# A graph network on one Trainium2 core: order of the first loads, places of side work in the first pairs, and the last pair's scores transposed by TensorE

## The chip, the core and the metric

The kernel runs on one core of a Trainium2 chip. The metric is device time in microseconds, lower is better: the median of three executions. A further execution was taken with the hardware profiler, and everything said about instructions comes from that one.

The engines are called as the profile calls them: PE (matmul; PEld is its weight load), DVE (VectorE), ACT (ScalarE), POOL (GpSimd), SP (SyncE, which here only issues DMAs). PSUM is the memory into which PE writes, SBUF the working memory.

## The reference

Two layers work on x of 64 x 256 x 512 with one 256 x 256 adjacency of zeros and ones. Cut to what is computed:

```
h   = relu(layernorm(x))
q, k, v = h Wq', h Wk', h Wv'
rel = adj' * (q k')                  # 256 x 256 per batch
rel = rel / norm(rel, axis=2)        # by row
x   = x + rel v
h   = relu(layernorm(x))
x   = x + (adj h) weight + bias
```

## The kernel before

**Tiling.** Two batches make a pair: 512 tokens, four chunks of 128 tokens on the partitions. There are 32 pairs, and x of a pair lives in one of five ring buffers of 1 MB. Wq and Wk are folded into one matrix m = Wq' Wk in `before_pairs`, so the scores are (h m) h'. Large products go through `winograd`: seven products of 2 x 2 blocks instead of eight, each of eight PE instructions, gathered in three PSUM banks (bank_a, bank_b, bank_c). After each product `take` moves its bank: the first time of a block as a copy on ACT, later as an add on DVE. The operands of products 3 to 7 are sums of blocks that DVE makes (`left_operands`, `right_operands`; four steps each). With `early=True` the product into bank_b is issued second instead of sixth.

**Stages of a pair.** `ln0` makes statistics (DVE) and relu (ACT). h is transposed: for pair 0 by PE (`transposes_by_matmul`), for later ones by 16 DMAs that place blocks of 32 (`place_blocks`, on SP) and DVE transposes within the blocks (`transpose_blocks`), then four sums. `project_g` is h m, `project_v` is h Wv'. `scores` makes rel; side steps mask it by adj' (DVE), make square sums (ACT), square root (ACT) and reciprocal (DVE), scale it (ACT), place it by 16 DMAs on SP, and turn it on DVE. `attend` multiplies turned rel with v and adds to x on DVE, `ln1` normalises again, `gather` multiplies with adj' and `mix` with the second weight and adds.

In `gather` h is split into an upper and a lower part of a shorter float type (`upper` on ACT, `lower` on DVE), which goes with `adjt_r`, adj' cast to that type. This is the branch for an adj whose values the short type holds exactly, chosen at run time: `look` masks the low bits of adj on DVE, reduces them, and leaves `low_any`, which all engines load before the branch.

**Order.** Everything from `before_pairs` on is issued in the order of the program on PE, DVE and ACT; no scheduler moves it. Each `winograd` takes a dict `side`: the steps in slot n are issued after the take of product n. So the place of a step in these dicts is its place in the queue of its engine. [...]

**Around the change.** SP issues wq in four pieces, then x of pair 0, wv, x of pairs 1 and 2, weight, x of pairs 3 and 4 (L99 to L113); ACT issues wk in four pieces; POOL issues adj first (L97) and the bias last (L114), and makes the identity between. `before_pairs` starts PE on 14 matmuls of zeros (L498), then makes the operands of m in the order of L541. The look and the transposes of adj stand in slot 2, those of Wv in slot 5. `first_pairs` is the hand-made order of pairs 0 to 3 until the steady loop can start: `attend(0)` is followed by `project_g(2)` with pair 1's masks and squares in its slots, the cast to `adjt_r` (L629), `gather(0)` with pair 3's sums, and `mix(0)` with `early=True`. `steady` is the loop over pairs 1 to 28. `last_pairs` does the rest: the last pair's scores are scaled and placed in slots of `mix(a)` (L696), turned in `gather(b)` (L697), and used by `attend(c)` (L699).

Of the kernel before, what the change touches and what calls it, by code (L numbers as in the profile page):

```python
# [9 lines left out]
F32 = mybir.dt.float32  # L10
# [9 lines left out]
def kernel(  # L20
# [36 lines left out]
    nc = tc.nc  # L57
# [27 lines left out]

    def load(i):
        X[i] = ring[i % len(ring)]
        nc.sync.dma_start(out=X[i], in_=xs[i])

# [6 lines left out]
    bias_bc = const.tile([P, D], F32, name="bias_bc")  # L96
    nc.gpsimd.dma_start(out=adj_sb, in_=adj.rearrange("(c p) n -> p c n", p=P))  # L97
    for e in range(DC):
        nc.sync.dma_start(out=wq_sb[:, e], in_=wq[e * P : (e + 1) * P, :])  # L99
        nc.scalar.dma_start(out=wk_sb[:, e], in_=wk[e * P : (e + 1) * P, :])  # L100
    ident = const.tile([P, P], F32, name="ident")
    make_identity(nc, ident)
    ones = const.tile([P, 1], F32, name="ones")
    nc.gpsimd.memset(ones, 1.0)
    warm = const.tile([P, P], F32, name="warm")
    nc.gpsimd.memset(warm, 0.0)
    load(0)
    nc.sync.dma_start(out=wv_sb, in_=wv.rearrange("(c p) d -> p c d", p=P))
    load(1)
    load(2)  # L110
    nc.sync.dma_start(out=w_sb, in_=weight.rearrange("(c p) d -> p c d", p=P))
    load(3)
    load(4)  # L113
    nc.gpsimd.dma_start(  # L114
        out=bias_bc, in_=bass.AP(tensor=bias.tensor, offset=bias.offset, ap=[[0, P], [1, D]])
    )

# [8 lines left out]
    def right_operands(b, t):  # L126

        sub = nc.vector.tensor_sub  # L130
        steps = [
            lambda: sub(t[1], b(1, 1), b(0, 1)),
            lambda: sub(b(0, 1), b(0, 1), b(0, 0)),
            lambda: sub(t[0], b(1, 1), b(0, 1)),
            lambda: sub(t[2], b(1, 0), t[0]),
        ]
        return {1: b(0, 0), 2: b(1, 0), 3: b(1, 1), 4: t[2], 5: b(0, 1), 6: t[0], 7: t[1]}, steps

# [77 lines left out]
    def product_of_tokens(left, right):  # L216

        def product(bank, n, start):
            for b in range(NB):
                for d in range(HC):  # L220
                    nc.tensor.matmul(  # L221
                        bank[:, ts(b, P)], right[n][:, d, ts(b, P)], left[n][:, d, ts(b, P)],
                        start=(start and b == 0 and d == 0), stop=(d == HC - 1),
                        skip_group_check=True,
                    )
        return product
# [111 lines left out]

    def scores(i, side={}):

# [43 lines left out]
        def each(f):  # L384
            return [(lambda b=b, k=k: f(b, k)) for k in range(NC) for b in range(NB)]

        winograd(product_of_tokens(left, right), take, side)
        return (
            [lambda: mask(0), lambda: mask(1)], each(square_sum), root, inverse, each(scale), place,
            each(turn),  # L390
        )

    def attend(i, side={}):
        rel, v, xt = R.pop(i), flat(V.pop(i)), flat(X[i])
        for b in range(NB):
            for n in range(NC):
                c = b * NC + n
                pm = ps_m.tile([P, 512], F32, tag="pm", name="pu")
                for m in range(NC):
                    nc.tensor.matmul(  # L400
                        pm[:, :D], rel[:, b, m, n], v[:, b * NC + m, :],
                        start=(m == 0), stop=(m == NC - 1),
                    )
                nc.vector.tensor_add(xt[:, c, :], pm[:, :D], xt[:, c, :])  # L404
                run(side.get(c, ()))
# [89 lines left out]
    def before_pairs():  # L495

        pz = ps_m.tile([P, 512], F32, tag="pm", name="pz")
        for _ in range(14):  # L498
            nc.tensor.matmul(pz[:, :P], warm, warm, start=True, stop=True)
        m_left, left_steps = left_operands(  # L500
            work, wq_sb.rearrange("p c (h n) -> p c h n", h=NC), "ys", "m"
        )
        wk_t = work.tile([P, 3, HC, HD], F32, tag="gt", name="wk_t")
        m_factors, right_steps = right_operands(right_blocks(wk_sb), [wk_t[:, n] for n in range(3)])
        low = work.tile([P, NC * N], I32, tag="h", name="low")
        stats, root, end, relus = ln0(0)
# [19 lines left out]
        def transpose_wv():  # L526
            for d in range(DC):
                pt = ps_m.tile([P, 512], F32, tag="pm", name="ptw")
                for e in range(DC):
                    nc.tensor.transpose(pt[:, ts(e, P)], wv_sb[:, e, ts(d, P)], ident)  # L530
                nc.scalar.copy(wvt_sb[:, d, :], pt[:, :D])

        def take(t, k, bank, first):
# [6 lines left out]

        run(left_steps[0:2] + right_steps[0:2])  # L541
        winograd(product_weights_moving(m_left, m_factors), take, {
            0: [],
            1: [left_steps[2], right_steps[2]],
            2: [left_steps[3], right_steps[3], look, transpose_adj],
            3: stats[0:2],
            4: stats[2:4] + [root],
            5: [end] + relus + m_steps[0:3] + [transpose_wv],
            6: m_steps[3:4],
# [31 lines left out]
    def first_pairs(exact):  # L581
# [5 lines left out]
        project_g(0, {  # L587
            0: stats[0:1], 1: stats[1:2], 2: stats[2:4] + [root], 3: [end] + relus,
            4: wv_steps[0:2], 5: wv_steps[2:3], 6: wv_steps[3:4],
# [23 lines left out]
        project_v(1, {  # L613
            0: gs[0:2], 1: gs[2:3] + turned2[0:2], 2: gs[3:4] + turned2[2:4], 3: turned2[4:6],
            4: turned2[6:8], 5: turns[0:2] + relus[0:2], 6: turns[2:4] + relus[2:4],
        })
# [4 lines left out]
        stats, *parts = ln1(0, exact)  # L621
        attend(0, {c: [stats[c]] for c in range(TC)})
        turned3, sums3 = transpose_blocks(3)
        project_g(2, by_slot(layer_1(parts), {
            0: masks[0:1], 1: masks[1:2], 2: squares, 3: [norm_root], 4: [inverse] + scales + [place],
            5: turned3[0:2], 6: turned3[2:6],
        }))
        if exact:
            nc.vector.tensor_copy(adjt_r, adjt_sb)  # L629
        y_steps = gather(0, exact, {0: turned3[6:8], 1: sums3[0:2], 2: sums3[2:3], 3: sums3[3:4]})  # L630
        stats, root, end, relus = ln0(4)
        mix(0, {
            0: y_steps[0:2], 1: y_steps[2:4], 2: stats[0:1], 3: stats[1:2], 4: stats[2:3],
            5: stats[3:4] + [root] + turns[0:2], 6: [end] + turns[2:4] + relus,
        }, early=True)
        place_blocks(4)
# [38 lines left out]
    def last_pairs(exact):  # L675
# [14 lines left out]
        }, tag="h")  # L690
        masks, squares, norm_root, inverse, scales, place, turns = scores(c)
        stats, *parts = ln1(b, exact)
        attend(b, by_slot({n: [stats[n]] for n in range(TC)}, {
            1: masks[0:1], 2: masks[1:2] + squares[0:2], 3: squares[2:4],
        }))
        mix(a, by_slot({0: [norm_root, inverse]}, layer_1(parts), {1: scales + [place]}))  # L696
        y_steps = gather(b, exact, {2: turns[0:2], 3: turns[2:4]})  # L697
        stats, *parts = ln1(c, exact)
        attend(c, {n: [stats[n], y_steps[n]] for n in range(TC)})  # L699
        mix(b, layer_1(parts))  # L700
        y_steps = gather(c, exact)
        mix(c, {0: y_steps[0:2], 1: y_steps[2:4]}, early=True)

# [35 lines left out]
```

## Time and profile before

| | us |
|---|---|
| median of three runs | 1773.24 (1772.54 to 1774.07) |
| the profiled execution | 1774.41 |
| its span, first to last instruction | 1772.6 |
| mean granted PE clock | 0.995 |
| PE busy in the span | 1741.8 |
| ACT busy / DVE busy | 645.9 / 1217.1 |

The span is what the profile divides; 1.8 us of the profiled execution lie around it. Busy times of different engines overlap. A busy PE isn't necessarily PE at full pace: where the granted clock falls, the same instruction takes longer. Bytes moved by DMA in the first fortieth of the span run at a mean of 225 GB/s, afterwards at 24 to 84. The chain that ended last is 94% PE.

### The profile page before, as it was taken

The numbers are of one execution on the slowest core, as the hardware profiler recorded it, in microseconds if no ns is written. First come the engines' busy times: TensorE is split into PE (matmuls) and PEld (weight loads), VectorE is DVE, ScalarE is ACT, GpSimd is POOL, SyncE is SP. The second block draws the span as 40 slices with busy tenths as digits, with TensorE's granted clock in tenths as the row PEclk, the third lists the DMA queues.
The fourth block names the chain that finished last, engine by engine and source line by source line (L and its number), as shares of the span: only waits on it lengthen the run. The fifth ranks groups of instructions, "written<-read, shape, count | busy, mean of one in ns | idle before, by whom it ended". The sixth has DMA issues, their size and how long they took to land.

```text
span 1772.6 us, 23888 instructions
## 1 busy us (share of the span) xinstructions
PE 1741.8 (98%) x8826; PEld 1452.6 (82%) x8826; DVE 1217.1 (69%) x2355; ACT 645.9 (36%) x1391; POOL 201.1 (11%) x169
## 2 busy tenths in 40 slices
PE   8989999999999999999999999999999999999988
PEld 6878888888888888888988888888888888888866
DVE  5767676667776667676667776676766676766545
ACT  3334333434333344242344233343333343333431
POOL 0011110111110111110111100111100111101111
PEclk9999999999999999999999999999999999999999
DMA  6423332233332233332333332333322333321111
GB/s 225 60 37 77 79 83 49 48 84 75 81 70 58 52 82 75 82 61 62 57 81 74 84 57 58 65 79 77 83 53 49 79 76 79 81 52 24 36 36 50
DMA packets 430062, 122.79 MB, mean 69 GB/s; under 512 B 402416, under 2 KB 403440, under 8 KB 429936
## 3 DMA queue, kind: packets, MB, share of 16 engines
q1 hardware_dynamic: 420768, 87.10, 25.9%
q0 software_dynamic: 8592, 33.03, 5.3%
q8 instruction: 71, 1.16, 0.3%
q10 hardware_dynamic: 576, 1.05, 0.2%
q14 instruction: 55, 0.45, 0.1%
HBM read 38.27 MB, written 33.55 MB: 41 GB/s over the span
## 4 chain that ended last, share of the span: by engine, by line
PE 94%; DVE 2%; ACT 1%; SPq 1%; DMA 1%; issue 1%; DVEq 0%; ACTq 0%
PE bank_a L209 25%; PE pu L400 12%; PE bank_c L209 12%; PE bank_a L197 12%; PE py L449 7%; PE bank_a L221 6%; PE bank_c L197 6%; PE bank_b L209 6%; PE bank_c L221 3%; PE bank_b L197 3%; PE bank_b L221 2%; SPq L379 1%; DMA wq_sb<-in_L_gnn_Wq_dram 0%; DVE st L240 0%; ACT h2c L252 0%
## 5 line engine op out<-in xcount | busy, mean ns | idle before, releaser
L400 PE MATMUL pu<-v,turned 128*128 128x512 f32 x512 | 229.4, 601 | 8.9 <-DVE turned L382 6.6
L422 POOL TENSOR_TENSOR x_ring<-x_ring,bias_bc 128x512 f32<-128x512 f32 x128 | 175.0, 1386 | 462.1 <-ACT h2c L252 462.1
L400 PEld LDWEIGHTS pu<-v,turned 128*128 128x128 f32 x512 | 95.5, 192 | 128.0 <-issue 108.6
L240 DVE BATCH_NORM_STATS2 st<-x_ring 128x6 f32<-128x512 f32 x256 | 176.1, 688 | 4.3
L333 ACT COPY v<-bank_a 128x512 f32<-128x512 f32 x96 | 56.0, 583 | 307.3 <-PE bank_a L209 301.0
L430 DVE TENSOR_TENSOR h<-h2c,h 128x512 fp32r<-128x512 f32 x128 | 122.5, 974 | 63.8 <-ACT h L426 63.8
L466 DVE TENSOR_TENSOR x_ring<-bank_a,x_ring 128x512 f32<-128x512 f32 x128 | 87.3, 682 | 90.5 <-PE bank_a L209 86.7
L473 POOL DMA_DIRECT2D out_dram<-x_ring x31 | 23.9, 770 | 1087.6 <-issue 834.9
L316 ACT COPY g<-bank_a 128x512 f32<-128x512 f32 x96 | 56.2, 585 | 220.1 <-PE bank_a L197 219.4
L449 PE MATMUL py<-adjt_r,h 128*128 128x256 f32 x1024 | 128.3, 284 | 3.9 <-DVE adjt_r L629 3.9
L449 PEld LDWEIGHTS py<-adjt_r,h 128*128 128x128 f32 x1024 | 122.8, 192 | 4.4 <-issue 4.3
L209 PE MATMUL bank_a<-w_t,ys 128*128 128x256 f32 x512 | 121.3, 380 | 1.1 <-DVE x_ring L466 1.1
L209 PE MATMUL bank_a<-wv_t,hs 128*128 128x256 f32 x512 | 120.9, 379 | 0.0
L197 PE MATMUL bank_a<-hs,m_t 128*128 128x256 f32 x512 | 120.9, 379 | 0.0
L245 ACT ACTIVATE rs<-rs 128x4 f32<-128x4 f32 x64 | 13.2, 206 | 278.5 <-DVE rs L244 278.5
L252 ACT ACTIVATE h<-x_ring,nb,rs 128x512 f32<-128x512 f32 x124 | 91.0, 803 | 51.4 <-DVE nb L249 51.4
L209 PEld LDWEIGHTS bank_a<-w_t,ys 128*128 128x128 f32 x512 | 97.0, 190 | 15.4 <-DVE x_ring L466 2.3
L404 DVE TENSOR_TENSOR x_ring<-pu,x_ring 128x512 f32<-128x512 f32 x128 | 88.4, 690 | 30.8 <-PE pu L400 23.3
L252 ACT ACTIVATE h2c<-x_ring,nb,rs 128x512 f32<-128x512 f32 x128 | 97.4, 806 | 29.6 <-DVE h L430 15.3
L209 PEld LDWEIGHTS bank_a<-wv_t,hs 128*128 128x128 f32 x512 | 97.3, 190 | 13.2
L197 PEld LDWEIGHTS bank_a<-hs,m_t 128*128 128x128 f32 x512 | 97.3, 190 | 13.2
L453 ACT COPY yt<-py 128x512 f32<-128x512 f32 x128 | 73.9, 578 | 40.6 <-PE py L449 40.6
(149 smaller groups left out, 3250.9 us busy)
## 6 DMA issues: line engine op xcount, KB each, us to landing
x_ring<-in_x_dram SPq DMA_DIRECT2D x32, 1024.0 KB, 5.6
blocks<-h SPq DMA_DIRECT2D x496, 64.0 KB, 2.3
out_dram<-x_ring POOLq DMA_DIRECT2D x31, 1024.0 KB, 5.2
placed<-rel SPq DMA_DIRECT2D x512, 32.0 KB, 2.0
wq_sb<-in_L_gnn_Wq_dram SPq DMA_DIRECT2D x4, 256.0 KB, 6.4
wk_sb<-in_L_gnn_Wk_dram ACTq DMA_DIRECT2D x4, 256.0 KB, 5.6
wv_sb<-in_L_gnn_Wv_dram SPq DMA_DIRECT2D x1, 1024.0 KB, 11.3
w_sb<-in_L_gnn_weight_dram SPq DMA_DIRECT2D x1, 1024.0 KB, 14.4
```

The source lines that it names most:

```text
L197: nc.tensor.matmul(bank[:, e * HT_ : (e + 1) * HT_], right[n][:, d, ts(e, P)], left[n][:, d, :], start=(start and e == 0 and d == 0), stop ...
L209: nc.tensor.matmul(bank[:, b * HD : (b + 1) * HD], left[n][:, d, ts(b, P)], right[n][:, d, :], start=(start and b == 0 and d == 0), stop=( ...
L221: nc.tensor.matmul(bank[:, ts(b, P)], right[n][:, d, ts(b, P)], left[n][:, d, ts(b, P)], start=(start and b == 0 and d == 0), stop=(d == H ...
L240: nc.vector.bn_stats(st[:, c, :], src[:, c, :])
L252: nc.scalar.activation(dst, src[:, c, :], AF.Relu, bias=nb[:, c : c + 1], scale=rs[:, c : c + 1])
L400: nc.tensor.matmul(pm[:, :D], rel[:, b, m, n], v[:, b * NC + m, :], start=(m == 0), stop=(m == NC - 1),)
L404: nc.vector.tensor_add(xt[:, c, :], pm[:, :D], xt[:, c, :])
L422: nc.gpsimd.tensor_tensor(xt[:, c, :], xt[:, c, :], bias_bc, ALU.add)
L430: nc.vector.tensor_sub(dst[:, 1, c, :], whole_h[c], dst[:, 0, c, :].bitcast(F32))
L449: nc.tensor.matmul(pm[:, d, :], left[:, b * NC + m, ts(d0 + d, P)], right, start=(n == 0), stop=(n == len(terms) - 1),)
L453: nc.scalar.copy(y[:, d0 : d0 + 2, :, b, :], pm.rearrange("p d (h n) -> p d h n", h=NC))
L466: nc.vector.tensor_add(xt[block], bank.rearrange("p (b e) -> p b e", b=NB), xt[block])
```

## The change

Five things change.

1. Loads. adj is issued by ACT ahead of wk. SP issues only wq and x of pair 0. wv, x of pairs 1 to 4, weight and bias are issued by ACT, from slots of the m product and of `project_g(0)`. POOL issues no load; it makes ones and the zeros for the warm matmuls first and the identity last.
2. The start of `before_pairs`. A square root of one number comes first on ACT. Eight warm matmuls instead of 14. The look and the transposes of adj come ahead of all operand steps. `right_operands` has a fourth buffer here, so its second step no longer overwrites a block of wk. Steps stand in other slots; of the four copies of Wv's transposes two are on ACT and two on DVE, and they stand ahead of the relus.
3. `first_pairs`. Two relus of pair 3 move from slots 5 and 6 to 2 and 3 of `project_v(1)`. Masks, squares and square root of pair 1 move from `project_g(2)` into `attend(0)`. The cast to `adjt_r` moves ahead of `project_g(2)`. Pair 3's DVE transposes start a slot earlier, its sums move from `gather(0)` to the last slot of `mix(0)`. `mix(0)` is no longer early; two of its operand steps come before it.
4. The last pair. `scores(c)` is not scaled, placed and turned; `turn_at_once` transposes it with eight PE transposes after `mix(a)`, and ACT copies the two banks. `attend(c)` multiplies by the reciprocal norm of the row in its add on DVE.
5. The last `mix` is no longer early; two of its operand steps come before it.

```diff
-    def load(i):
+    def load(i, queue=nc.sync):
         X[i] = ring[i % len(ring)]
-        nc.sync.dma_start(out=X[i], in_=xs[i])
+        queue.dma_start(out=X[i], in_=xs[i])
...
-    nc.gpsimd.dma_start(out=adj_sb, in_=adj.rearrange("(c p) n -> p c n", p=P))
+    nc.scalar.dma_start(out=adj_sb, in_=adj.rearrange("(c p) n -> p c n", p=P))
     for e in range(DC):
         nc.sync.dma_start(out=wq_sb[:, e], in_=wq[e * P : (e + 1) * P, :])
         nc.scalar.dma_start(out=wk_sb[:, e], in_=wk[e * P : (e + 1) * P, :])
-    ident = const.tile([P, P], F32, name="ident")
-    make_identity(nc, ident)
+    load(0)
...
-    load(0)
-    nc.sync.dma_start(out=wv_sb, in_=wv.rearrange("(c p) d -> p c d", p=P))
-    load(1)
-    load(2)
-    nc.sync.dma_start(out=w_sb, in_=weight.rearrange("(c p) d -> p c d", p=P))
-    load(3)
-    load(4)
-    nc.gpsimd.dma_start(
-        out=bias_bc, in_=bass.AP(tensor=bias.tensor, offset=bias.offset, ap=[[0, P], [1, D]])
-    )
+    ident = const.tile([P, P], F32, name="ident")
+    make_identity(nc, ident)
+
+    def load_wv():
+        nc.scalar.dma_start(out=wv_sb, in_=wv.rearrange("(c p) d -> p c d", p=P))
+
+    def load_w_and_bias():
+        nc.scalar.dma_start(out=w_sb, in_=weight.rearrange("(c p) d -> p c d", p=P))
+        nc.scalar.dma_start(
+            out=bias_bc, in_=bass.AP(tensor=bias.tensor, offset=bias.offset, ap=[[0, P], [1, D]])
+        )
...
+        diff = t[3] if len(t) > 3 else b(0, 1)
         steps = [
             lambda: sub(t[1], b(1, 1), b(0, 1)),
-            lambda: sub(b(0, 1), b(0, 1), b(0, 0)),
-            lambda: sub(t[0], b(1, 1), b(0, 1)),
+            lambda: sub(diff, b(0, 1), b(0, 0)),
+            lambda: sub(t[0], b(1, 1), diff),
             lambda: sub(t[2], b(1, 0), t[0]),
         ]
...
+        def turn_at_once():
+            for b in range(NB):
+                pt = ps_m.tile([P, T], F32, tag="pm", name="pr")
+                for t in range(NC):
+                    for k in range(NC):
+                        nc.tensor.transpose(
+                            pt[:, ts(t * NC + k, P)], rel[:, b, k, ts(t, P)], ident
+                        )
+                nc.scalar.copy(turned[:, b].rearrange("p t k n -> p (t k n)"), pt)
...
-                nc.vector.tensor_add(xt[:, c, :], pm[:, :D], xt[:, c, :])
+                if scale is None:
+                    nc.vector.tensor_add(xt[:, c, :], pm[:, :D], xt[:, c, :])
+                else:
+                    nc.vector.scalar_tensor_tensor(
+                        xt[:, c, :], pm[:, :D], scale[:, b, n : n + 1], xt[:, c, :],
+                        op0=ALU.mult, op1=ALU.add,
+                    )
...
+        root_table = small.tile([P, 1], F32, tag="rt", name="root_table")
+        nc.scalar.activation(root_table, ones, AF.Sqrt)
         pz = ps_m.tile([P, 512], F32, tag="pm", name="pz")
-        for _ in range(14):
+        for _ in range(8):
...
-        wk_t = work.tile([P, 3, HC, HD], F32, tag="gt", name="wk_t")
-        m_factors, right_steps = right_operands(right_blocks(wk_sb), [wk_t[:, n] for n in range(3)])
-        low = work.tile([P, NC * N], I32, tag="h", name="low")
+        wk_t = work.tile([P, 4, HC, HD], F32, tag="h", name="wk_t")
+        m_factors, right_steps = right_operands(right_blocks(wk_sb), [wk_t[:, n] for n in range(4)])
+        low = work.tile([P, NC * N], I32, tag="rel", name="low")
...
-                nc.scalar.copy(wvt_sb[:, d, :], pt[:, :D])
+                if d < HC:
+                    nc.scalar.copy(wvt_sb[:, d, :], pt[:, :D])
+                else:
+                    nc.vector.tensor_copy(wvt_sb[:, d, :], pt[:, :D])
...
-        run(left_steps[0:2] + right_steps[0:2])
+        look()
+        transpose_adj()
+        run([right_steps[1], left_steps[0], left_steps[1]])
         winograd(product_weights_moving(m_left, m_factors), take, {
-            0: [],
+            0: [load_wv],
             1: [left_steps[2], right_steps[2]],
-            2: [left_steps[3], right_steps[3], look, transpose_adj],
-            3: stats[0:2],
-            4: stats[2:4] + [root],
-            5: [end] + relus + m_steps[0:3] + [transpose_wv],
+            2: stats[0:2] + [lambda: load(1, nc.scalar)],
+            3: [left_steps[3]] + stats[2:4] + [root, right_steps[0], lambda: load(2, nc.scalar)],
+            4: [transpose_wv, end] + relus + [right_steps[3]],
+            5: m_steps[0:3],
             6: m_steps[3:4],
         }, early=True)
...
         project_g(0, {
-            0: stats[0:1], 1: stats[1:2], 2: stats[2:4] + [root], 3: [end] + relus,
+            0: stats[0:1] + [lambda: load(3, nc.scalar)],
+            1: stats[1:2] + [lambda: load(4, nc.scalar)],
+            2: stats[2:4] + [root, load_w_and_bias], 3: [end] + relus,
...
-            0: gs[0:2], 1: gs[2:3] + turned2[0:2], 2: gs[3:4] + turned2[2:4], 3: turned2[4:6],
-            4: turned2[6:8], 5: turns[0:2] + relus[0:2], 6: turns[2:4] + relus[2:4],
+            0: gs[0:2], 1: gs[2:3] + turned2[0:2], 2: gs[3:4] + turned2[2:4] + relus[0:2],
+            3: turned2[4:6] + relus[2:4], 4: turned2[6:8], 5: turns[0:2], 6: turns[2:4],
...
-        attend(0, {c: [stats[c]] for c in range(TC)})
+        attend(0, by_slot({c: [stats[c]] for c in range(TC)}, {
+            0: masks[0:1], 1: masks[1:2] + squares[0:2], 2: squares[2:4] + [norm_root],
+        }))
         turned3, sums3 = transpose_blocks(3)
-        project_g(2, by_slot(layer_1(parts), {
-            0: masks[0:1], 1: masks[1:2], 2: squares, 3: [norm_root], 4: [inverse] + scales + [place],
-            5: turned3[0:2], 6: turned3[2:6],
-        }))
         if exact:
             nc.vector.tensor_copy(adjt_r, adjt_sb)
-        y_steps = gather(0, exact, {0: turned3[6:8], 1: sums3[0:2], 2: sums3[2:3], 3: sums3[3:4]})
+        project_g(2, by_slot(layer_1(parts), {
+            1: [inverse], 3: scales + [place], 4: turned3[0:1], 5: turned3[1:2], 6: turned3[2:4],
+        }))
+        y_steps = gather(0, exact, {0: turned3[4:6], 1: turned3[6:7], 2: turned3[7:8]})
+        run(y_steps[0:2])
         stats, root, end, relus = ln0(4)
         mix(0, {
-            0: y_steps[0:2], 1: y_steps[2:4], 2: stats[0:1], 3: stats[1:2], 4: stats[2:3],
-            5: stats[3:4] + [root] + turns[0:2], 6: [end] + turns[2:4] + relus,
-        }, early=True)
+            0: y_steps[2:3], 1: y_steps[3:4] + stats[0:1], 2: stats[1:2], 3: stats[2:3],
+            4: stats[3:4] + [root], 5: [end] + turns + relus, 6: sums3,
+        })
...
-        masks, squares, norm_root, inverse, scales, place, turns = scores(c)
+        masks, squares, norm_root, inverse, rn, turn_at_once = scores(c, by_matmul=True)
...
-        mix(a, by_slot({0: [norm_root, inverse]}, layer_1(parts), {1: scales + [place]}))
-        y_steps = gather(b, exact, {2: turns[0:2], 3: turns[2:4]})
+        mix(a, by_slot({0: [norm_root, inverse]}, layer_1(parts)))
+        turn_at_once()
+        y_steps = gather(b, exact)
         stats, *parts = ln1(c, exact)
-        attend(c, {n: [stats[n], y_steps[n]] for n in range(TC)})
+        attend(c, {n: [stats[n], y_steps[n]] for n in range(TC)}, rn)
         mix(b, layer_1(parts))
         y_steps = gather(c, exact)
-        mix(c, {0: y_steps[0:2], 1: y_steps[2:4]}, early=True)
+        run(y_steps[0:2])
+        mix(c, {0: y_steps[2:4]})
```

More of the change, by code (lines that the diff above doesn't have):

```diff
@@ L130, in right_operands @@
         sub = nc.vector.tensor_sub
+        diff = t[3] if len(t) > 3 else b(0, 1)
         steps = [
             lambda: sub(t[1], b(1, 1), b(0, 1)),
-            lambda: sub(b(0, 1), b(0, 1), b(0, 0)),
-            lambda: sub(t[0], b(1, 1), b(0, 1)),
+            lambda: sub(diff, b(0, 1), b(0, 0)),
+            lambda: sub(t[0], b(1, 1), diff),
             lambda: sub(t[2], b(1, 0), t[0]),
         ]
-        return {1: b(0, 0), 2: b(1, 0), 3: b(1, 1), 4: t[2], 5: b(0, 1), 6: t[0], 7: t[1]}, steps
+        return {1: b(0, 0), 2: b(1, 0), 3: b(1, 1), 4: t[2], 5: diff, 6: t[0], 7: t[1]}, steps
     def weight_operands(w, name):
@@ L337, in project_v, with scores @@
         winograd(product_weights_moving(HL[i], wv_right), take, side)
-    def scores(i, side={}):
+    def scores(i, side={}, by_matmul=False):
         left, right = HL.pop(i), G.pop(i)
@@ L385, in each @@
             return [(lambda b=b, k=k: f(b, k)) for k in range(NC) for b in range(NB)]
+        def turn_at_once():
[7 more added lines that the diff above has]
+                nc.scalar.copy(turned[:, b].rearrange("p t k n -> p (t k n)"), pt)
         winograd(product_of_tokens(left, right), take, side)
+        if by_matmul:
+            masks = [lambda: mask(0), lambda: mask(1)]
+            return masks, each(square_sum), root, inverse, rn, turn_at_once
         return (
@@ L391, in scores, with attend @@
         )
-    def attend(i, side={}):
+    def attend(i, side={}, scale=None):
         rel, v, xt = R.pop(i), flat(V.pop(i)), flat(X[i])
```

## The prediction, made before the result was known

> **What bounds the kernel now.** I read first the busy shares, then the list of what the matrix engine (PE) waited for, then PE's instructions in order of time at the head, around pair 0's second layer and at the end, and last the chain of waits and the clock table there. The page:
>
> ```profile
> span 1772.6 us, 23888 instructions
> PE 1741.8 (98%) x8826; PEld 1452.6 (82%) x8826; DVE 1217.1 (69%) x2355; ACT 645.9 (36%) x1391; POOL 201.1 (11%) x169
> ```
>
> PE is the bound, so only time in which PE stands still or runs slowly can be won. The waits of PE over the whole run (total, times, longest):
>
> ```profile
> PE pu L400 <- DVE turned L382: 6.6, 2, 6.2
> PE py L449 <- DVE adjt_r L629: 3.9, 1, 3.9
> PE bank_a L209 <- DVE x_ring L466: 2.7, 5, 0.8
> PE pf L514 <- DVE low_max L512: 2.1, 1, 2.1
> PE bank_c L209 <- DVE yt L159: 1.2, 2, 0.6
> ```
>
> Nothing here repeats by pair: the long waits happen once each, outside the steady loop. PE in order of time (start, duration, what; the bracket is the idle time before):
>
> ```profile
> 17.84 3.45 PE L209 MATMUL bank_a<-wk_t,ys_m 128*128 128x256 f32 x8
> 117.76 6.52 PE L449 MATMUL py<-adjt_r,h 128*128 128x256 f32 x32 [3.91 <-DVE adjt_r L629]
> 163.48 3.90 PE L449 MATMUL py<-adjt_r,h 128*128 128x256 f32 x32
> 1726.48 9.39 PE L400 MATMUL pu<-v,turned 128*128 128x512 f32 x16 [6.20 <-DVE turned L382]
> 1764.83 1.99 PE L209 MATMUL bank_a<-w_t,yt 128*128 128x256 f32 x8 [0.78 <-DVE x_ring L466]
> ```
>
> A product of 8 matmuls normally follows the last by 1.73 us; the one at 17.84 took 3.3, pair 0's gather 6.4 against 3.7 for the same 32 matmuls at 163.48, the last attend 9.2 against 6.87. Each follows a pause. The clock column shows why (PE, PEld, DVE, ACT, POOL busy, then granted clock):
>
> ```profile
> 118.00:120.00 2.00, 2.00 (x10) 2.00 (x11) 1.93 (x4) 0.15 (x1) 0.00 (x0) 0.50 0.40 55
> 1728.00:1730.00 2.00, 2.00 (x3) 0.67 (x2) 0.00 (x0) 0.00 (x0) 0.00 (x0) 0.50 0.00 0
> ```
>
> So a pause costs its length and some 1.5 to 2.6 us of half clock after it. The chain of waits at the head (start, us, what):
>
> ```profile
> 2.18 8.66 DMA wq_sb<-in_L_gnn_Wq_dram
> ...
> 26.53 2.22 ACT blocks L252 x3
> ...
> 29.37 1.86 ACT wvt_sb L531 x4
> ...
> 31.74 2.08 ACT ht L281 x4
> ```
>
> After the last piece of wq (10.84) DVE does its subtractions, then the look at adj, and PE stands behind it; at the end ACT is the bound: four relus, four wvt copies, four ht copies in a row.
>
> [...]
>
> **Head.** In PE's order the products of m = wq'wk write bank_a, bank_b, bank_c, then bank_a, bank_c, bank_a, bank_a again; s and t are the sums of wq and wk that DVE makes for them. Arrivals: about 2.5 MB lie ahead of the last weight piece before and after (adj leaves POOL's queue and goes ahead of wk on ACT's; bias goes away), so that piece still lands at about 10.9 and bank_b, which needs it, still ends at 12.5. adj now has the place of wk's first piece (shortest landing 3.8 us): about 4.6. The look (0.42 + 0.69), its small matmul and four transposes (0.83) end by 7, before bank_a's weights (wk's second piece, some 7.7): hidden, with 1.3 us to spare. In the compiled order wk's fourth issue on ACT waits for adj's completion counter; nothing on ACT is due before 6.9. Then, with a DVE pitch of 0.6 to 0.7, 1.65 for two stats and 1.73 for a product, bank_c starts at 12.5 behind bank_b, no longer at 13.04 behind wk's in-place subtraction, and ends at 14.25.
>
> DVE makes the add of bank_b by 13.4, s[1] by 14.0 and t[0] by 14.65, so the second bank_a product runs from 14.75 to 16.5 (before 17.84 to 21.1, behind the look and at half clock). Two stats end at 16.3, s[2] at 16.95; the second bank_c product runs from 17.05 to 18.8, wv's 16 transposes to 20.7, the last two products to 22.4 and 24.3.
>
> DVE goes on with two stats, the root's input and t[1] to 19.4, the add to 20.0, two wvt copies to 21.6, reciprocal and nb to 21.95. ACT has made the other two wvt copies by 20.6; its relus take 22.0 to 24.9, m_sb ends at 25.5, then ht comes. Before, four wvt copies stood between relus and m_sb.
>
> The first ht copy starts at 25.5, not 31.74: 6.2 us. wv is issued on ACT at some 10.5, behind x0: 2.6 us at 400 GB/s and a landing make 15.5; due 18.8. x1 to x4, w and bias are issued in ACT's waits, 0.4 to 0.5 us each as wk's issues. The table load at 21.93 lay in a wait: 0. Six warm matmuls fewer: 0, or one product at half clock (1.5). Bounds 3.7 (that, and the last piece 1 us later) to 7.5 (that piece 1.3 us earlier).
>
> **Pairs 0 to 2.** Moving two relus of pair 3 ahead removes PE's 0.56 us at 90.14. From project_g(2) at 101.58 to attend(1) at 138.10 are 36.5 us; at full pace 12.1 + 3.7 + 12.1 = 27.9. So 8.6 + 0.56 = 9.2 is there. With adjt_r cast before project_g(2), and squares out of ACT's way, the last low part of h2 is done about when gather starts and half a gather before it is needed; gather runs at full clock. The order of mix(0) changes too: bank_b's product goes from second to sixth, which takes away the 0.61 and 0.78 us waits; the second yt step is done 0.8 us after gather, 1.7 allowed. What is late next: (a) two masks (0.58 each) and the cast (0.32) now sit between attend(0)'s adds and ln1(0): the last pair's attend with two masks ended 0.7 us later than one without; with the cast 1.06, less 0.37 that the square root waited anyway, 0.7. ACT's copy of the second bank of project_g(2) stands behind two relus, and PE's fourth product waits for it: 0.6. (b) The four sums of pair 3 (2.75 us) now stand on DVE between the last take of mix(0) and attend(1)'s adds, after four turns (1.4): DVE reaches the first add 2.3 us late, catches up 0.1 per chunk, and project_v(2)'s fourth product waits about 2.0, as its copy before was just in time (150.1 against 150.19). 9.2 - 0.6 - 2.0 = 6.6. Bounds 4.0 (both stalls double) to 9.2. SP's placing of pair 1 may meet the end of w's load: up to 0.4, within these.
>
> **End.** Removed: four scales on ACT (1.7), sixteen placings on SP (12.6, in the chain from 1711.96 to 1726), four turns. Added: eight PE transposes at 0.12 (ptw: 16 in 1.91) = 0.96 before gather(b), two ACT copies of 0.58 beside the gather. attend(c) starts at 1716.29 + 0.96 + 3.73 = 1720.98 (before 1726.48) at full clock. DVE, not PE, is now late: per chunk add, stats, aggregate, one y step = 2.13 us, so the last y step ends at 1731.5, the take of mix(b)'s first bank at 1732.2; PE wanted that bank at 1731.3: 0.9 of stall instead of the 0.26 before. From there mix(b) repeats the trace (9.27 us to gather(c)): gather(c) at 1741.5 (before 1748.85), mix(c) at 1745.3. There the order with bank_b sixth and two y steps before it has no stall: last take 12.35 us after its start, against 14.19. The last take falls from 1766.87 to 1757.7: 9.2. Bounds: 7.2 if the fused add takes 1.2 us (4 x 0.5), 10.9 if mix(b) waits nowhere (0.9, and 0.7 before its fifth product).
>
> **Sum.** 6.2 + 6.6 + 9.2 = 22.0 of the profiled execution's 1774.41 (span 1772.6, 1.8 around it): 1752.4. The runs' median lies 1.2 lower, 1773.24: 1751.2. The steady loop's PE order and side work are unchanged: 0.
>
> **Rivals.** (1) The stalls come back in part, because the moved work lands where slack is nothing: every lower bound at once, 3.7 + 4.0 + 7.2 = 14.9, 1758.3. For: project_v's copies are just in time already. Against: the steady loop lives with that. (2) More than I count: no new stalls, 27.6, about 1746; against it the DVE rows in (b). (3) Slower: ACT, which evicts most PSUM banks, is held at each load it issues until the load before has landed. Two of SP's loads took 4.11 us and two 7.29 to issue. Six 1 MB loads move to ACT, wv in a wait of 4.5 us, so five count; at the 5.6 us that an x load takes to land, 28.0, and 28.0 - 22.0 = 6.0 slower: 1779.2. It decides from 4.4 us a load. Against: [...] and they are spaced 1.7 us or more. That the change does not do what it says: the instruction lists of all engines show the moved steps, so no.
>
> **How the numbers follow.** Forecast 0.60; rival 1 0.27; rival 2 0.07; rival 3 0.04; 0.02 for no change. Bounds give 1745.6 to 1758.3; for what rival 1 leaves beyond them I take 1745.5 to 1760. A measurement here tells 0.2% (3.5 us) from nothing. Faster 0.94, same 0.02, slower 0.04.
>
> **What would show it.** Right: the first ht copy near 25.5; a gather of pair 0 of 3.7 us with no adjt_r wait; a new wait of about 2 us in project_v(2); pr transposes of about 1 us, then attend(c) in 6.9 us. Wrong: load issues on ACT of over 2 us, half clock in the head, or DVE copies that hold the relus past 23.

## The result and the profile after

| | before | after |
|---|---|---|
| median of the runs | 1772.95 us (4 runs, 1772.54 to 1774.07) | 1753.03 us (4 runs, 1751.17 to 1755.15) |
| profiled execution | 1774.41 us, span 1772.6 | 1753.72 us, span 1751.9 |

The ratio is 0.9887, 95% interval 0.9870 to 0.9904: 19.9 us less, where 22.0 were forecast. The page of the kernel after:

```profile
span 1751.9 us, 23847 instructions
PE 1734.2 (99%) x8822; PEld 1447.8 (83%) x8822; DVE 1216.7 (69%) x2353; ACT 644.6 (37%) x1387; POOL 199.4 (11%) x167
```

PE is still the bound. Of the 20.7 us that the span is shorter, only 7.6 are busy time; the rest is idle time. The waits of PE in the kernel after (total, times, longest):

```profile
PE bank_a L210 <- DMA wk_sb<-in_L_gnn_Wk_dram: 1.9, 1, 1.9
PE bank_a L210 <- DVE x_ring L487: 1.8, 3, 0.9
PE bank_c L210 <- ACT v L334: 1.2, 1, 1.2
PE pf L537 <- DVE low_max L535: 1.2, 1, 1.2
PE pu L415 <- DVE turned L384: 0.9, 2, 0.4
```

The 6.2 us for `turned` and the 3.9 for `adjt_r` are gone. What stands first now was not on the list before: wk's second piece, in the head. PE of the kernel after in order of time, with the places shown of before and the new waits:

```profile
8.81 2.90 PE L210 MATMUL bank_a<-wk_sb,wq_sb 128*128 128x256 f32 x6 [1.91 <-DMA wk_sb<-in_L_gnn_Wk_dram]
11.50 3.28 PE L210 MATMUL bank_b<-wk_sb,wq_sb 128*128 128x256 f32 x8
16.93 1.97 PE L210 MATMUL bank_a<-wk_t,ys_m 128*128 128x256 f32 x8 [0.42 <-DVE wk_t L135]
109.32 3.99 PE L470 MATMUL py<-adjt_r,h 128*128 128x256 f32 x32
138.99 1.99 PE L210 MATMUL bank_c<-wvt_sb,hs 128*128 128x256 f32 x8 [1.21 <-ACT v L334]
152.29 3.89 PE L470 MATMUL py<-adjt_r,h 128*128 128x256 f32 x32
1704.73 1.04 PE L394 MATMUL pr<-ident,rel 128*128 128x128 f32 x8
1709.38 7.03 PE L415 MATMUL pu<-v,turned 128*128 128x512 f32 x16
1720.77 1.99 PE L210 MATMUL bank_a<-w_t,ys 128*128 128x256 f32 x8 [0.91 <-DVE x_ring L487]
```

Pair 0's gather takes 3.99 us instead of 6.52, attend(c) 7.03 instead of 9.39; the product at 16.93 has its full pace again. But two products at 8.81 and 11.50 now run at half pace (2.90 us for 6 records, 3.28 for 8; at full pace 8 take 1.89). The clock table of the kernel after says the same (the number behind POOL's is the granted clock):

```profile
9.00:10.00 1.00, 1.00 (x3) 0.82 (x4) 1.00 (x2) 0.00 (x0) 0.00 (x0) 0.50 1.06 410
110.00:112.00 2.00, 2.00 (x20) 2.00 (x19) 2.00 (x7) 1.35 (x3) 0.00 (x0) 1.00 0.38 51
1710.00:1712.00 2.00, 2.00 (x6) 0.80 (x5) 0.70 (x1) 0.16 (x1) 0.00 (x0) 1.00 0.11 43
```

Full clock in the gather and in the last attend; half clock in the head. Its chain of waits, kernel after:

```profile
1.75 6.92 DMA wk_sb<-in_L_gnn_Wk_dram
8.67 0.14 issue
8.81 2.90 PE bank_a L210 x6
11.71 3.09 PE bank_b L210 x8
...
22.43 1.29 DVE wvt_sb L557 x2
...
25.34 1.99 PE bank_a L210 x8
```

The chain now runs over PE and DVE; the relus and wvt copies of ACT that stood in it before are gone from it.

The same milestones in both traces show where the time came from (starts, us):

| milestone | before | after | gained so far |
|---|---|---|---|
| first ht copy | 31.74 | 28.01 | 3.7 |
| gather of pair 1 | 163.48 | 152.29 | 11.2 |
| gather of pair 29 | 1662.71 | 1650.85 | 11.9 |
| gather of the last pair | 1748.85 | 1730.04 | 18.8 |
| last take | 1766.87 | 1746.16 | 20.7 |

With the end of project_g(0) as the border (its last product starts 3.8 us earlier) that is 3.8 for the head, 7.4 for pairs 0 to 2, 0.7 in the loop and 8.9 at the end, against a forecast of 6.2, 6.6, 0 and 9.2. Three questions follow: are the parts independent, why is the head short, and what are the new waits worth?

### The profile page after: what moved, and what is told of

Same layout as the page of the kernel before. It is cut to its first block, busy times and chain, and to the rows that moved or that the text cites. A ratio compares the mean times of both kernels' runs of the same rounds, so it can differ in the third digit from the quotient of the medians.

```text
span 1751.9 us, 23847 instructions
## 1 busy us (share of the span) xinstructions
PE 1734.2 (99%) x8822; PEld 1447.8 (83%) x8822; DVE 1216.7 (69%) x2353; ACT 644.6 (37%) x1387; POOL 199.4 (11%) x167
## 4 chain that ended last, share of the span: by engine, by line
PE 95%; DVE 3%; ACT 0%; DMA 0%; issue 0%; ACTq 0%; DVEq 0%
PE bank_a L210 25%; PE bank_a L198 12%; PE bank_c L210 12%; PE pu L415 12%; PE py L470 7%; PE bank_a L222 7%; PE bank_b L210 6%; PE bank_c L198 6%; PE bank_c L222 3%; PE bank_b L198 3%; PE bank_b L222 2%; DVE st L241 1%; DMA wk_sb<-in_L_gnn_Wk_dram 0%; DVE x_ring L420 0%; DVE x_ring L487 0%
## 5 line engine op out<-in xcount | busy, mean ns | idle before, releaser
L302 DVE STREAM_TRANSPOSE ht<-blocks 128x256 f32<-128x256 f32 x248 | 87.2, 408 | 1.1 <-DMA blocks<-h 1.1
```

The lines of the kernel that those rows point to most:

```text
L302: nc.vector.transpose(ht[:, d, half].rearrange("p (b n) -> p b n", b=NB), by_half[:, :, half, d])
```

## The experiments

All ratios are to runs of the kernel before on the same chip (its medians there: 1774.71, 1774.49 and 1775.40 us).

**The three parts alone.** The kernel before with one part of the diff each.

> Only the head part (loads behind one another on ACT, adj looked at first, fourth buffer for wk's differences, two wvt copies on DVE); side work of pairs 0 to 2 and the last pair as before. Theory (three independent parts, the head's worth read at the first ht copy): 3.8 us below the kernel before, about 1769.1. Rival (the head's gain is taken back later, because the loads of x1 to x4 now come later): less than 2 us. Rival (the forecast's 6.2 is there and what hid it was elsewhere): 6 us.

> Only the other places for side work of pairs 0 to 2, head and last pair as before. Theory: gain 7.4 us (my forecast counted 6.6): gather of pair 0 without the wait for adjt_r and in about 4.0 us, a wait of project_v(2)'s fourth product of about 1.2. Rival (part of the 7.4 belongs to the head, because loads shifted): under 5.

> Only the last pair's part: its scores turned by PE, the fused multiply-add in attend(c), the last mix not in early order. Theory: gain 9.0 us, fused add 0.75, attend(c) 7.0 without a wait, one wait of 0.9 before mix(b)'s third product. Rival (the tail's gain depends on the rest): more than 2 us away from 9.0. The sum of this and the two others is to be the change's whole 19.9 to 20.7 if the parts are independent.

| part alone | median, us | below before | ratio, 95% interval |
|---|---|---|---|
| head | 1770.46 | 4.3 | 0.9977 (0.9969 to 0.9986) |
| pairs 0 to 2 | 1768.47 | 6.2 | 0.9965 (0.9952 to 0.9979) |
| last pair | 1765.74 | 9.0 | 0.9950 (0.9937 to 0.9964) |

They sum to 19.5 us; the whole change gave 19.9, and 21.4 when it was run again. So they are independent within what these runs tell. The end alone also shows the forecast's path step by step: the last gather starts at 1741.45 and the last take at 1757.70, where 1741.5 and 1757.7 were forecast. Head and pairs give 0.3 and 0.9 us less alone than their own traces show at the gather of pair 1 (4.6 and 7.1). One reason can be read, though it was not tried: both keep the last pair's placing by DMA, and attend(c) waits 6.9 and 6.8 us for it there, 6.2 in the one profile of before. Scatter is as large: the runs of the head alone reach from 1768.07 to 1772.81.

**The clock in the head.** The six warm matmuls that the change takes away, put back:

```diff
-        for _ in range(8):
+        for _ in range(14):
```

> The kernel after, with 14 warm matmuls again in place of 8. Theory (the head fell 2.4 us short of my forecast because fewer warm matmuls, then idle time behind 4.5 and 6.9 us, let PE's clock fall to half for bank_a and bank_b): both at full clock, bank_b's product ends near 12.7 instead of 14.8, first ht copy near 26.0 instead of 28.0, 1.7 to 2.1 us below the kernel after (about 1751.2). Rival (the weights' landing is the bound, the clock only fills the wait): bank_b ends at 14 or later, no gain. Rival (more warm matmuls only delay the look at adj behind them): up to 1 us slower.

Measured: 1752.92 us, ratio 0.9879 (0.9863 to 0.9894). PE of this kernel:

```profile
1.04 5.93 PE L522 MATMUL pz<-warm 128*128 128x128 f32 x28 [1.04 <-POOL warm L105]
...
7.51 1.89 PE L210 MATMUL bank_a<-wk_sb,wq_sb 128*128 128x256 f32 x8
9.24 0.59 PE L210 MATMUL bank_b<-wk_sb,wq_sb 128*128 128x256 f32 x2
10.41 1.56 PE L210 MATMUL bank_b<-wk_sb,wq_sb 128*128 128x256 f32 x6 [0.58 <-DMA wk_sb<-in_L_gnn_Wk_dram]
```

Both products at full pace, bank_b done at 11.97 instead of 14.78, the first ht copy at 25.20 instead of 28.01: the trace is as the clock theory expects. It also shows what the weights allow: bank_b waits for wk's last piece until 10.41. But the total fell by less than 2.8 us, and the interval overlaps that of the kernel after: the runs alone don't show a gain, the trace does. The next question is whether 28.01 is typical.

**The kernel after once more.**

> The kernel after itself, for a second profile of it and a common base for the three others. Five kernels so far share its head (the part alone and three edits elsewhere among them), and their first ht copies came at 25.3, 25.3, 26.1, 26.9 and 28.0 us. Theory (when PE's clock leaves half speed behind eight warm matmuls and the idle time after them differs by run): ht's first copy anywhere from 25.3 to 28.0, runs spread by 2 us or more, mean granted clock between 0.997 and 0.999. Rival (28.0 belongs to this kernel): 28.0 again, and a spread under 1 us.

Measured: 1754.04 us (1753.03 to 1755.07), ratio 0.9888 (0.9871 to 0.9904); first ht copy at 26.04. PE of this second profile:

```profile
1.03 3.60 PE L522 MATMUL pz<-warm 128*128 128x128 f32 x16 [1.03 <-POOL warm L105]
5.88 0.19 PE L537 MATMUL pf<-ones,low_max 128*1 128x1 f32 x2 [1.24 <-DVE low_max L535]
6.00 0.66 PE L544 MATMUL pta<-ident,adj_sb 128*128 128x128 f32 x4
6.49 0.60 PE L210 MATMUL bank_a<-wk_sb,wq_sb 128*128 128x256 f32 x2
8.01 2.90 PE L210 MATMUL bank_a<-wk_sb,wq_sb 128*128 128x256 f32 x6 [0.92 <-DMA wk_sb<-in_L_gnn_Wk_dram]
10.70 2.12 PE L210 MATMUL bank_b<-wk_sb,wq_sb 128*128 128x256 f32 x8
```

Its clock table:

```profile
7.00:8.00 1.00, 0.09 (x1) 0.02 (x1) 0.03 (x1) 0.28 (x1) 0.00 (x0) 0.87 1.06 377
11.00:12.00 1.00, 1.00 (x5) 0.82 (x5) 0.00 (x0) 0.53 (x1) 0.00 (x0) 0.93 0.23 82
```

wk's second piece let bank_a go on at 8.01, not 8.81, and the clock came back inside bank_b's product, shortly after 11 us. So one program has several heads.

The first products show how. In this profile and the first one, PE had reached full pace: adj's four transposes took 0.66 us, as with 14 warm matmuls, and bank_a's first two records 0.60. It lost it again while PE stood still. The shares 0.87 and 0.93 above, worked out, put the half clock at 7.74 to 11.14 us; the same working on the first profile (0.74 in 7:8, 0.85 in 14:15) gives 7.48 to 14.30. So half clock lasted 3.4 us here and 6.8 there. Ahead of the fall PE stood still from 4.63 to 5.88 and from 7.09 on, 1.25 and 0.65 us; in the first profile it was 1.18 and 0.58. One pause of that size alone brought no fall: behind the 1.21 us at 138.99 (first profile) and the 1.39 us at 14.19 (adj on POOL's queue, below) eight records took 1.99 and 1.89 us. What else the fall depends on is not shown. In the profile of the head alone the same records ran at half pace, so there PE had not yet reached full pace:

```profile
5.58 1.12 PE L544 MATMUL pta<-ident,adj_sb 128*128 128x128 f32 x4
6.49 1.06 PE L210 MATMUL bank_a<-wk_sb,wq_sb 128*128 128x256 f32 x2
```

Six profiles share this head (this one, the first, the head alone, and three edits elsewhere, below): 28.01, 26.04, 26.87, 25.36, 26.07, 25.32, mean 26.28. Three profiles with the head of before show 31.74, 31.91 and 31.74. The head's gain is thus 5.5 us in the mean, 3.7 to 6.4 by profile; the profile of after caught the least. My rival that 28.0 belongs to the kernel falls. With 14 warm matmuls two profiles lie together, at 25.20 and 25.13 (the second is the combined kernel below): putting them back is worth about 1.1 us of the mean. Their four runs each lie within 0.5 and 1.2 us, the eight of the kernel after within 4.0; but two kernels below with eight warm matmuls have four runs each within 0.8 and 1.0, so the spread of runs proves little.

**The order of the first loads.** adj back on POOL's queue and looked at behind bank_c's product:

```diff
-    nc.scalar.dma_start(out=adj_sb, in_=adj.rearrange("(c p) n -> p c n", p=P))
+    nc.gpsimd.dma_start(out=adj_sb, in_=adj.rearrange("(c p) n -> p c n", p=P))
...
-        look()
-        transpose_adj()
...
-            2: stats[0:2] + [lambda: load(1, nc.scalar)],
+            2: [look, transpose_adj] + stats[0:2] + [lambda: load(1, nc.scalar)],
```

> The kernel after, with adj back on POOL's queue and looked at behind bank_c's product, as in the kernel before; all else of the head as after. Theory (looking first takes 1.1 us of DVE and the wait of PE for it out of the chain): PE waits again some 1 to 2 us for the look, ht's first copy 1 to 2 us later than in the kernel after, total 1 to 2 above it. Rival (adj ahead of wk delays wk by as much as it brings): no difference.

Measured: 1752.14 us, ratio 0.9878 (0.9863 to 0.9893), first ht copy at 25.79: no loss. PE:

```profile
2.46 3.78 PE L522 MATMUL pz<-warm 128*128 128x128 f32 x16 [2.46 <-POOL warm L105]
6.03 2.94 PE L210 MATMUL bank_a<-wk_sb,wq_sb 128*128 128x256 f32 x8
8.80 2.28 PE L210 MATMUL bank_b<-wk_sb,wq_sb 128*128 128x256 f32 x8
...
14.19 0.19 PE L537 MATMUL pf<-ones,low_max 128*1 128x1 f32 x2 [1.39 <-DVE low_max L535]
```

The wait for the look is back (1.39 us), as my theory said. But without adj ahead of it wk lets bank_a run through from 6.03, with no pause behind the warm matmuls. What looking first saves, loading adj first takes back: the rival holds, within limits. The edit also starts the warm matmuls 1.4 us later, without a pause behind them, and 25.79 is one profile beside six that differ by 2.7 us. The other half of that part, loads one behind the other, was undone with adj left first: wv, x1 to x4, w and the bias all issued on SP behind x0.

```diff
     load(0)
+    nc.sync.dma_start(out=wv_sb, in_=wv.rearrange("(c p) d -> p c d", p=P))
+    load(1)
+    load(2)
...
```

> The kernel after with wv, x1 to x4, w and the bias issued at once on SP behind x0, as in the kernel before, instead of one behind the other on ACT; adj and the look stay. Theory (my forecast: x0 is still in flight when the last piece of wk lands, so what is queued behind x0 does not matter to the weights): wk and wq land as in the kernel after, ht's first copy between 25.3 and 28.0, total within 1 us of it. Rival (the staggered issues are part of the head's gain): wk's second or last piece lands 1 us or more later, ht's first copy at 28 or later, total over 1.5 above.

Measured: 1753.09 us, ratio 0.9881 (0.9865 to 0.9898), the wait for wk's second piece ends at 7.79, first ht copy at 25.84. The staggering by itself shows no gain here.

**The sums of pair 3.**

```diff
-            4: stats[3:4] + [root], 5: [end] + turns + relus, 6: sums3,
+            4: stats[3:4] + [root], 5: [end] + turns + relus,
...
-        masks, squares, norm_root, inverse, scales, place, turns = scores(i + 1)
+        masks, squares, norm_root, inverse, scales, place, turns = scores(i + 1, {0: more[0:2], 1: more[2:4]})
```

(`more` is `sums3` for the first steady pair, and nothing for the others.)

> The kernel after, with the four sums of pair 3 moved from behind mix(0) into scores(2), where DVE stood idle for 2.85 us. Theory (the 1.2 us wait of project_v(2)'s fourth product comes from DVE reaching attend(1)'s adds late behind these sums): the wait goes, from attend(1) to gather(1) 25.4 us instead of 26.8, total 1.2 to 1.4 below the kernel after. Rival (the wait comes from the layer-1 relus on ACT and DVE's first adds in general): the wait stays at over 0.8.

Measured: 1751.94 us, ratio 0.9879 (0.9863 to 0.9894). PE of this kernel:

```profile
122.85 7.10 PE L415 MATMUL pu<-v,turned 128*128 128x512 f32 x16
...
134.97 1.97 PE L210 MATMUL bank_c<-wvt_sb,hs 128*128 128x256 f32 x8
...
148.27 3.89 PE L470 MATMUL py<-adjt_r,h 128*128 128x256 f32 x32
```

No wait before the fourth product; attend(1) to gather(1) takes 25.42 us, 26.80 in the kernel after. The wait was the sums' doing, as forecast. The 1.4 us are read from the trace; the interval of the runs overlaps that of the kernel after, as it does for the next edit.

**The last pair.** First, mix(b)'s late takes:

```diff
-        attend(c, {n: [stats[n], y_steps[n]] for n in range(TC)}, rn)
-        mix(b, layer_1(parts))
+        attend(c, {n: [stats[n]] + y_steps[0:3][n : n + 1] for n in range(TC)}, rn)
...
+            0: [root, y_steps[3], end, relus[0], relus[1]],
+            1: [uppers[0], uppers[1]],
+            2: [lowers[0], relus[2], lowers[1]],
```

> The kernel after, with the fourth y step of the last but one pair moved from attend(c) into mix(b)'s first slot, and the first low part of h2 put behind the third product's take there. Theory (mix(b)'s third and fifth products wait 0.91 and 0.45 us because DVE's takes stand behind that step and that low part): waits of about 0.3 and 0, from attend(c) to gather(c) 19.7 us instead of 20.66, total 0.9 to 1.0 below the kernel after. Rival (h2 then comes late for gather(c)): a new wait before gather(c), gain under 0.3.

Measured: 1751.96 us, ratio 0.9876 (0.9861 to 0.9891). PE waits 0.32 us before the third product and not at all before the fifth; attend(c) to gather(c) takes 19.35 us (1708.79 to 1728.14) instead of 20.66, 0.3 better than expected.

Then the turning itself, back to ACT, SP and DVE with plain adds, the last mix left as in the kernel after:

```diff
-        masks, squares, norm_root, inverse, rn, turn_at_once = scores(c, by_matmul=True)
+        masks, squares, norm_root, inverse, scales, place, turns = scores(c)
...
-        turn_at_once()
-        y_steps = gather(b, exact)
+        y_steps = gather(b, exact, {2: turns[0:2], 3: turns[2:4]})
```

> The kernel after, with the last pair's scores scaled by ACT, placed by SP's sixteen DMAs and turned by DVE as in the kernel before, and plain adds in attend(c); the last mix stays as in the kernel after. Theory (the end's 9.0 us are about 7.2 from the turning and 1.8 from the order of the last mix): attend(c) waits some 6 us for the turned scores and runs at half clock behind that, total 7.2 above the kernel after. Rival (most of it was the order of the last mix): under 5 above.

Measured: 1760.17 us, ratio 0.9923 (0.9909 to 0.9936). PE:

```profile
1702.34 4.12 PE L470 MATMUL py<-adjt_r,h 128*128 128x256 f32 x32
1713.23 8.69 PE L415 MATMUL pu<-v,turned 128*128 128x512 f32 x16 [6.76 <-DVE turned L384]
```

The wait (6.76 us) and the slow attend behind it (8.69 us, 7.03 in the kernel after) are back. Between pair 29 and the last gather this kernel loses 7.5 us to the kernel after (7.2 expected); by the ratios of the runs it is 6.2 to 6.4. The rest of the end's 9.0 is the last mix: 12.3 us from its start to its last take, 14.2 before.

**What beats both.** Two combinations, on the chip that ran the kernel after again:

> The kernel after with 14 warm matmuls, pair 3's sums in scores(2), and mix(b)'s fourth y step and first low part put later. Theory (the three are independent): 1.3 for the head's mean, 1.3 and 1.0 as their traces showed, 3.6 below the kernel after. Rival (the head's gain is within the scatter): 2.3.

> The same without adj ahead of wk: adj on POOL's queue, the look on DVE while it waits for wq, the small matmul and adj's transposes behind bank_b's product, 12 warm matmuls. Theory (adj ahead of wk cost bank_a's start as much as looking first brought; a look in DVE's idle time costs neither): bank_a's product from about 7, no wait of PE for the look, ht's first copy near 24.3, another 0.8 to 1.2 below the version with 14 warm matmuls. Rival (the wait for wq's last pieces sets bank_b either way): no difference between the two.

| kernel | median (range), us | ratio, 95% interval |
|---|---|---|
| after, again | 1754.04 (1753.03 to 1755.07) | 0.9888 (0.9871 to 0.9904) |
| 14 warm, sums and mix(b) moved | 1750.25 (1749.63 to 1750.78) | 0.9864 (0.9848 to 0.9881) |
| 12 warm, adj not first, sums and mix(b) moved | 1749.47 (1748.77 to 1749.69) | 0.9861 (0.9844 to 0.9877) |

The first is 3.8 us below the kernel after (3.6 expected), the second 4.6; the intervals of the ratios overlap, the runs' ranges against the kernel after do not. PE of the second in the head:

```profile
6.95 1.89 PE L210 MATMUL bank_a<-wk_sb,wq_sb 128*128 128x256 f32 x8
...
9.56 1.53 PE L210 MATMUL bank_b<-wk_sb,wq_sb 128*128 128x256 f32 x6 [0.28 <-DMA wq_sb<-in_L_gnn_Wq_dram]
11.02 0.19 PE L539 MATMUL pf<-ones,low_max 128*1 128x1 f32 x2
```

The look lies in DVE's wait for wq, and PE does not wait for it; the first ht copy starts at 24.36. Between the two combinations 0.8 us are as expected in size, but their ranges touch: that step is only likely.

## Why the prediction was right, and where not

**Right**: faster, and 1753.03 against 1751.2, inside the range. In the pairs and at the end the mechanism was as described: pauses of PE go, and with each the half clock behind it (granted clock 0.50 in 118:120 and 1728:1730 before, 1.00 in 110:112 and 1710:1712 after). In the head it was so only in part: "half clock in the head" stood among the signs of being wrong, and it came.

**Pairs 0 to 2**, 7.4 against 6.6. All 9.2 us forecast as there came, and both new stalls came where they were placed, smaller: (a) 0.4 instead of 0.6, (b) 1.4 instead of 2.0. In (b) DVE reached the first add 2.2 us late, where 2.3 were forecast; but it then catches up 0.2 us a chunk (it needs 1.53, PE 1.74), not 0.1. Moving the sums removed (b) and nothing else.

**End**, 8.9 to 9.0 against 9.2. The turned attend, the 0.9 us wait and the last mix without a stall are as forecast. The fused multiply-add from PSUM took 0.75 us, not the 0.69 of a plain add: four times 0.06.

**Head**, 3.7 in the profiled execution and 5.5 in the mean of six, against 6.2. The first ht copy was forecast near 25.5; five of six profiles lie between 25.3 and 26.9. Three terms of that sum were off:

- "Six warm matmuls fewer: 0, or one product at half clock (1.5)", taken as 0. It is about 1.1 us in the mean, and up to 2.8: parts of two products at half clock, not one (in the first profile 2.90 us for six records of bank_a and 3.28 for eight of bank_b, where eight take 1.89). What it should have asked is where PE pauses: eight warm matmuls end at 4.5 us, and PE then waits for the look and for wk. The forecast read half clock behind pauses of 2.1, 3.9 and 6.2 us; what it did not do is add up short ones, which here came to 1.9 us before the clock fell (1.25 and 0.65 us in the second profile). It called the 1.3 us to bank_a's weights "to spare"; PE stood still there for 0.4 to 1.9 us. The number of slow matmuls differs by run: full pace came for good at 9.7 us, within bank_a's product, in two of the six heads and only at 14.3, at the end of bank_b's, in another. What decides between them is not shown.
- "that piece still lands at about 10.9 and bank_b ... still ends at 12.5". Where the clock did not hide it, wk's last piece let PE go on at 10.35 to 10.41, and bank_b ended at 11.9 to 12.0: about 0.5 us better than forecast, which gave back part of the first error.
- "hidden, with 1.3 us to spare" of the look put first: it is hidden, but adj takes wk's place, and bank_a went on only at 7.9 to 8.8 where it could run from 6.0. The net is nothing that these profiles show, where the forecast counted on the look leaving the chain as a gain.

The head of before as a whole is 5.5 us longer, yet neither loading and looking at adj first nor the staggered loads bring it. By the traces it is the rest: PE's wait of 2.1 us for the look with 1.6 of half clock behind it (0.50 granted from 18 to 20 us), the in-place subtraction on wk that held bank_c (0.53), the wvt copies on ACT between relus and m_sb, and last pieces of wq and wk that let PE go on 0.6 (adj first) to 1.4 us (adj on POOL's queue) sooner. That split was read, not tried piece by piece, and what the fourth buffer, the early square root and the wvt copies on DVE are worth each is open.

**Rivals.** Rival 3, ACT held at each load it issues, is out: in the kernel after, ACT's issues of wv, x1 to x4 and w took 0.37 to 0.39 us each, the bias 0.52. Only wk's fourth issue stood until adj had landed, as forecast: adj, issued at 0.75, landed 3.7 us later, and that issue began at 4.5. What made SP's issues of before long is not shown: three took 3.58, 4.59 and 2.65 us, and the last two ended at 15.6 and 18.3, long after the last piece of wq (10.84). Rival 1 had the sign of the error right (1758.3 against 1751.2), but not the cause: stalls in pairs and end were smaller than forecast, and the shortfall lies in the head.

**The loop**, forecast 0, measured 0.7: scatter. From the gather of pair 1 to that of pair 29 all fourteen profiles run the same loop, in 1498.6 to 1500.7 us (mean 1499.8); the profile of after has the shortest, 1498.56, before 1499.23. So the profiled execution of after had an unlucky head and a lucky loop, and its sum came out near the truth partly by that. Where in the loop the 0.1 us steps arise is open.

**A reading.** The prediction takes 400 GB/s for wv issued by ACT. The kernel before shows 379 to 410 by single microseconds from 10 to 28 us, but from 11 us on only SP's loads were in flight there. The kernel after shows it for ACT: wv, alone in flight, came at 375 and 412 GB/s between 14 and 16 us.

## What to carry to other kernels

In this kernel warm matmuls were not filler that may be cut down to what the loads need: behind eight of them pauses of 1.25 and 0.65 us came before half clock, behind 14 the products kept full pace (first ht copy at 25.2 us, against 26.3 in the mean of six). So add up the pauses between the last of them and the first real product, however short each is, and try what keeping PE busy across them brings. Putting one load first moves the loads behind it (adj first: bank_a went on at 7.9 to 8.8 us, where it could run from 6.0); ask what the displaced one starts. One profiled execution is one draw of the clock in a head (here 25.3 to 28.0 us for the first ht copy): before explaining a start by it, compare it with every other profile that shares that code.

## What was not expected of the hardware

The clock column shows 1.00 from the first microsecond of before and after, but the matmuls do not run so: the first warm matmuls there take 0.23 us a record, later transposes of that size 0.12. With adj on POOL's queue the column stays at 1.00 from 6 to 9 us while bank_a's product takes 2.94 us for its eight records, where 1.89 is full pace. In these heads durations tell the pace better than the clock column.

In seven profiles PE had no pause until full pace came; by the durations of the records I estimate 3.0 to 5.7 us after its start. With eight warm matmuls, adj first and pauses of 0.4 to 1.9 us behind them (seven profiles) there were two courses. In four, full pace came by 5.6 us and was lost again: at 7.5 us for 6.8 (first profile), at 7.7 for 3.4 (second), at about 8.4 for 3.4 (mix(b)'s takes moved, an estimate from the records' durations), and with the loads up front between 6.7 and 7.8, where PE stood still, until about 11.0. In three it first came, by the durations, at 9.7, 9.7 and 12.7 us.

In the head of before the transfers fall to 309 and 191 GB/s at 7 to 9 us; in the kernel after they are 365 and 336 there (first profile) and 377 and 381 (second). Two loads that differ can be set aside: with wv, x1 and x2 issued up front, as before, the kernel after still has 375 and 324, and with adj back on POOL's queue 377 and 375. What is left is the bias on POOL's queue, which reads one row for all 128 partitions. It was not tried by itself, so the cause is open.
